# Norm and rotary embedding of q and k joined, with wo and rotary tables loaded per layer and a refitted planner, in a two-layer transformer kernel

## The chip, the cores and the metric

The kernel runs on one core of one Trainium2 chip. The metric is device time in microseconds (us), the median of several executions. The engines of the core are TensorE (matmul; PE in the profile, its weight loads PEld), VectorE (DVE), ScalarE (ACT), GpSimd (POOL) and SyncE (SP), which issues nearly all DMA transfers.

## The reference

The input `x` has 8 sequences of 512 tokens and 256 channels, in float32. Three stages follow one another, each on the layer norm of `x`; the first and the last are the same two-layer network with the same weights:

```python
x = x + 0.5 * ffn(layernorm(x))          # two layers
x = x + global_attention(layernorm(x))   # 16 heads of 16, softmax(y y^T / 4) x, then @ weight
x = x + 0.5 * ffn(layernorm(x))          # the same two layers again

def layer(x):                            # DIM 256, 8 heads of 64, window 128
    h = shift_token(x)                   # second half of the channels from the token before
    q, k, v = split(h @ wqkv)            # 3 x 512
    q = l2norm(q) * q_scale; k = l2norm(k) * k_scale     # per head of 64
    q = q*cos*s + rotate_half(q)*sin*s;  k = k*cos/s + rotate_half(k)*sin/s
    o = local_attention(q, k, v)         # own window and the one before, causal
    x = x + o @ wo
    h = layernorm(shift_token(x)) * g + b
    a, gate = split(h @ w1 + b1)         # 2 x 682
    return x + (a * gelu(gate)) @ w2 + b2
```

## The kernel before, in words

**Streams.** Each of the 8 sequences is a block of 512 tokens, cut into 4 tiles of 128. A block passes twice through the two layers, once before and once after the global attention. Two streams (`k` = 0 and 1) each take 8 such passes in the order of `pairs`, so 16 layers each, 32 in all. A third stream, `global_stream`, does the 16 global heads of each block once its first pass is done. The streams are Python generators that record operations between `yield`s; the first stream starts `LAG` = 6 yields ahead of the second. One layer has 12 yields of attention and 6 of the gated network (`glu`).

**One layer's attention.** `front(t)` makes q, k and v of tile t: three matmuls with `wqkv`, a copy of each from PSUM on ScalarE, and for q and k apart the square (ScalarE), the sum per head and a maximum (VectorE), the power -0.5 (GpSimd, in `rn`), two products with the sine table for the rotated halves (GpSimd, in `t2`), the product with the cosine table, the sum of both, and for k the product with its norm (VectorE). q's norm is applied later, as the scale of the exponential. `scores(t)` multiplies q with the keys of the own and the previous tile, in two groups `g` of 4 heads; VectorE adds the mask and takes the peak, ScalarE takes the exponential and its sum, and the result `pg` is divided by the sum. `values(t)` multiplies it with v, `project(t)` with `wo`. The program order is front(0), then for each t: scores(t), project(t-1), front(t+1), values(t).

**Near and far.** Before the products, q and k and then the probabilities must be transposed. In a stream's first and last pass ("near") TensorE does it, through PSUM. In the six passes between ("far", `FAR and 0 < n < len(blocks) - 1`) VectorE transposes blocks of 32 x 32 and a round trip through DRAM moves the blocks (`turned_far`, `turned_quarters`); there are 24 far layers with 96 tiles and 8 near ones with 32. Scores and values are matmuls of 64 rows that run side by side in the array.

**The order of work.** Nothing is issued as it is recorded. `Plan` records every operation, prices it (`cost`: how long the engine is held, and when the result is there), and `order` writes one list schedule for all engines: of the operations that can start first on an engine, the one of the lowest rank (its place in the recording) goes first, with a bonus of `STICK` ranks for a TensorE operation in the same array mode, and `MODE` ns charged for a change of it. Buffers are rings: a tile takes a slot when its first user is placed, and its slot comes free after its last one, so the planner decides the waits for buffers too. DMAs share one modelled `pipe` of 170 GB/s. The engines then run their own lists in order. As every operation goes through a recorder, nearly all of them have one line (L369) in the profile, and must be told apart by their tiles.

**Buffers and weights.** `wqkv`, `wo` and the rotary tables (times `qk_scales`) of both layers are loaded at the start and stay in SBUF; `w1`, `ends` and `w2` have one buffer and are loaded again for each step by `load_glu`. `qn` (q or k of a tile) has two buffers of 512 numbers per partition and stream; `glu` uses them too.

Of the kernel before, what the change touches and what calls it, by code (L numbers as in the profile page):

```python
# [15 lines left out]
P = 128  # L16
B, N, D = 8, 512, 256
NT = N // P
# [151 lines left out]
def elements(a):  # L170
    n = 1
    for d in a.shape[1:]:
        n *= d
    return n


class Plan:
# [55 lines left out]
    def cost(self, op):  # L233

        if op.engine == "tensor":

            lanes, op.mode = {}, "whole"
            for name, args, kw in op.calls:
                lane, t = 0, 109.0
                if name == "matmul":  # L240
                    a = kw["lhsT"]
                    lane, t = (a.region()[0], args[0].region()[0]), 2 * max(0.842 * elements(kw["rhs"]), 0.852 * a.shape[1])
                    k, m = a.shape
                    op.mode = "fours" if k <= 32 else "quarters" if k <= 64 and m <= 64 else "halves" if k <= 64 else "columns" if m <= 64 else "whole"
                lanes[lane] = lanes.get(lane, 0.0) + t
            busy = max(lanes.values())
            return busy, busy + 170
        name, args, kw = op.calls[0]
        n = max(elements(a) for a in (*args, *kw.values()) if hasattr(a, "shape"))
        if name == "dma_start":  # L250
            return 580.0, 2300.0
        if op.engine == "scalar":
            if name == "activation":
                op.mode = {AF.Exp: "exp", AF.Gelu: "gelu"}.get(args[2])
                busy = 70 + 0.82 * n + (105 if "bias" in kw else 0)
                return (busy + 93, busy + 310) if "accum_out" in kw else (busy, busy + 110)
            return 70 + 0.81 * n, 175 + 0.81 * n
        if op.engine == "vector":
            if name == "tensor_tensor_reduce":
                return 90.0 + n, 250.0 + n  # L260
            if name == "bn_stats":
                return 70.0 + n, 150.0 + n
            return 90 + 1.035 * n, 170 + 1.035 * n
        if name == "memset":
            return 80 + 0.85 * n, 100 + 0.85 * n
        if ALU.pow in args:
            return 350.0 + 157 * n, 400.0 + 157 * n
        return 210 + 1.98 * n, 250 + 1.98 * n

    def order(self):  # L270
# [19 lines left out]
        pipe = 0.0  # L290
# [17 lines left out]
        while len(order) < len(self.ops):  # L308
# [31 lines left out]
            if op.calls[0][0] == "dma_start":  # L340
                a = op.calls[0][2]["out"]
                pipe = max(pipe, op.start + 2000.0) + elements(a) * a.shape[0] * 4 / 170
                op.end = pipe + 300
# [32 lines left out]
def macaron(ctx: ExitStack, tc: tile.TileContext, x, weight, wqkv, wo, w1, w2, b2, vecs, qk_scales, rotary, out):  # L376
# [16 lines left out]
    def load_attention(l):  # L393

        wq = wpool.tile([P, 2, 3 * INNER], F32, tag=f"wqkv{l}", name=f"wqkv{l}")
        for part in range(3):
            cols = slice(part * INNER, (part + 1) * INNER)
            nc.sync.dma_start(out=wq[:, :, cols], in_=wqkv[l, :, cols].rearrange("(k p) f -> p k f", p=P))
        o = wpool.tile([P, NPAIR, D], F32, tag=f"wo{l}", name=f"wo{l}")
        nc.sync.dma_start(out=o, in_=wo[l].rearrange("(k p) f -> p k f", p=P))  # L400
        return wq, o
# [23 lines left out]
    attention_weights = [load_attention(0)]  # L425
    glu_weights = [load_glu(0)]
    attention_weights.append(load_attention(1))
    tabs, vec = [], []
    for l in range(DEPTH):
        tab = const.tile([P, NT, 2, 2, DH], F32, tag=f"tab{l}", name=f"tab{l}")  # L430
        nc.scalar.dma_start(out=tab.rearrange("p t a s d -> p (t a s d)"), in_=rotary)
        sc = zpool.tile([P, 2, 2, DH], F32, tag=f"z{l}", bufs=2, width=N + 1)
        nc.scalar.dma_start(out=sc.rearrange("p a s d -> p (a s d)"), in_=qk_scales[l : l + 1, :].partition_broadcast(P))
        ve = const.tile([P, NVEC], F32, tag=f"vec{l}", name=f"vec{l}")
        nc.scalar.dma_start(out=ve, in_=vecs[l])
        vec.append(ve)
        for t in range(NT):
            nc.gpsimd.tensor_mul(tab[:, t], tab[:, t], sc)
        tabs.append(tab)
# [19 lines left out]
    nhalf = const.tile([P, HEADS], F32, tag="nhalf")  # L459
# [69 lines left out]
    def quarter_buffers():  # L529

        zeros = work.tile([P, 2 * P], F32, tag="t2", bufs=2, width=N)
# [24 lines left out]
    def later(k):  # L556

        if k not in later_of:
            zeros = work.tile([1, P], F32, tag="t2", bufs=2, width=N)
# [6 lines left out]
    def attention(k, y, l, far):  # L566
        wqkv_sb, wo_sb = attention_weights[l]
# [4 lines left out]
        v = {}  # L572
# [3 lines left out]
        def front(t):  # L576
# [4 lines left out]
            tb = tabs[l][:, t]  # L581
            pair = []
            for part in range(3):
# [6 lines left out]
                if part == 2:  # L590
                    vt = work.tile([P, INNER], F32, tag=f"v{k}", bufs=3)
                    nc.scalar.copy(vt, ps)
                    v[t] = vt
                    continue


                qk = work.tile([P, HEADS, 2, half], F32, tag=f"qn{k}", bufs=2)
                flat = qk.rearrange("p h a d -> p (h a d)")
                nc.scalar.copy(flat, ps)
                sq = work.tile([P, HEADS, DH], F32, tag="sq", bufs=1)  # L600
                nc.scalar.activation(sq.rearrange("p h d -> p (h d)"), flat, AF.Square)
# [28 lines left out]
        def scores(t, pair, rn):  # L630
# [21 lines left out]
            for g in range(2):  # L652
# [16 lines left out]
                with plan.together():  # L669
                    for i in range(2):  # L670
                        keys = kT[:, 2 * g + i].rearrange("p j k -> p (j k)")
                        for q, to, ks in sorted(pieces, key=lambda piece: piece[1].start - piece[1].stop):
                            for par in range(2):
# [3 lines left out]
                                )  # L677
                heads = slice(4 * g, 4 * g + 4)
# [53 lines left out]
        def values(t, probs):  # L732
# [25 lines left out]
            if far:  # L758
                for g in range(2):
                    with plan.together():  # L760
                        for i in range(2):
# [3 lines left out]
                            )  # L765
            else:
# [40 lines left out]

    def glu(k, y, step, xb, far):
# [3 lines left out]
        if far:  # L812
            sh = work.tile([P, NT, P], F32, tag=f"qn{k}", bufs=2)
# [40 lines left out]
        for m in range(FULL):  # L854
# [4 lines left out]
            else:  # L859
                u = work.tile([P, N], F32, tag=f"qn{k}", bufs=2)  # L860
# [14 lines left out]
        u = work.tile([P, N], F32, tag=f"qn{k}", bufs=2)  # L875
# [49 lines left out]
    def stream(k, blocks):  # L925

        for n, (b, second) in enumerate(blocks):
# [211 lines left out]
```

## Time and profile before

| | |
|---|---|
| median of 3 runs | 3949.23 us (3947.79 to 3949.27) |
| the profiled execution's own time | 3952.0 us |
| its span, first to last instruction | 3950.1 us |
| mean granted TensorE clock | 0.994 |
| instructions | 72878 |
| DMA | 400.74 MB, mean 101 GB/s |

A page of the profile gives the busy time of each engine and its share of the span, the span in 40 slices, the DMA queues, the chain of waits that ended last, and the groups of instructions. A group names engine, operation, tiles (`out<-in`), shapes and count, then busy time in us and the mean of one in ns, and behind the second bar the idle time before it and what ended it. A table of stretches gives, for each from:to in us, its length, the busy time of the engines with instruction counts, the granted clock and the DMA share. A line of the timeline gives start, duration, engine, tiles, shape and count.

### The profile page before, as it was taken

How to read it: one execution, taken by the hardware profiler on the slowest of the kernel's cores; microseconds unless marked ns; L12 is line 12 of the kernel's file. 1: busy time of each engine (PE TensorE's matmuls, PEld its weight loads, DVE VectorE, ACT ScalarE, POOL GpSimd, SP SyncE). 2: the span in 40 equal slices, each digit the busy share in tenths (PEclk: the TensorE clock that was granted, in tenths of full speed). 3: DMA queues.
4: the chain of work that ended last, by engine and by line, in shares of the span. 5: the costliest groups of instructions: out<-in, count | busy, mean ns of one | idle time of the engine just before them, and what ended most of it. 6: DMA issues, size and time to landing. Idle time of an engine off the chain costs nothing.

```text
span 3950.1 us, 72878 instructions
## 1 busy us (share of the span) xinstructions
PE 3878.5 (98%) x26240; PEld 2659.5 (67%) x26240; DVE 2447.9 (62%) x6888; ACT 1766.9 (45%) x4548; POOL 1233.7 (31%) x1132
## 2 busy tenths in 40 slices
PE   8999999999999999999999999999999999999998
PEld 4566776766767667677676776767767667686665
DVE  7676655667566665674765747657466565535674
ACT  5565534535344353452443534535335353324564
POOL 6242323424133341341422405324133242103240
PEclk9999999999999999999999999999999999999999
DMA  3000543534435344253442534525335244110000
GB/s 116 1 24 27 155 135 104 150 98 140 129 104 153 93 128 143 88 165 92 128 138 94 155 104 130 159 91 156 91 116 157 81 143 134 61 33 9 1 24 11
DMA packets 437644, 400.74 MB, mean 101 GB/s; under 512 B 53954, under 2 KB 379172, under 8 KB 437284
## 3 DMA queue, kind: packets, MB, share of 16 engines
q1 hardware_dynamic: 436420, 394.76, 33.5%
q8 instruction: 208, 3.41, 0.4%
q10 hardware_dynamic: 864, 1.33, 0.1%
q14 instruction: 152, 1.25, 0.1%
HBM read 235.49 MB, written 143.66 MB: 96 GB/s over the span
## 4 chain that ended last, share of the span: by engine, by line
PE 81%; DVE 5%; issue 2%; ACT 2%; POOL 1%; DMA 0%; SPq 0%; DVEq 0%; POOLq 0%; ACTq 0%
PE psum_bank L369 81%; ACT work_p L369 2%; DVE work_p L369 2%; DVE work_qn L369 1%; DVE small_ss L369 1%; POOL small_rn L369 0%; POOL work_t L369 0%; ACT work_both L369 0%; DVE work_xw L369 0%; DVE small_bnst L369 0%; SPq L369 0%; DVE work_both L369 0%; DVE work_o L369 0%; DVE xpool_x L369 0%; POOL small_rstd L369 0%
## 5 line engine op out<-in xcount | busy, mean ns | idle before, releaser
L369 PE MATMUL psum_bank<-work_xw,work_e 128*128 128x256 f32 x4096 | 960.0, 385 | 3.0 <-ACT work_e L369 1.9
L369 PEld LDWEIGHTS psum_bank<-work_xw,work_e 128*128 128x128 f32 x4096 | 765.8, 191 | 199.0 <-issue 47.2
L369 PE MATMUL psum_bank<-wpool_wqkv,zpool_z 128*128 128x512 f32 x1536 | 712.2, 603 | 2.7 <-ACT work_v L369 2.0
L369 ACT ACTIVATE work_p<-work_p,small_nmax,small_rn 128x192 f32<-128x192 f32 (+2 forms) x1024 | 543.7, 533 | 324.2 <-DVE small_nmax L369 213.7
L369 POOL TENSOR_TENSOR work_t<-work_qn,const_tab 128x256 f32<-128x256 f32 x512 | 397.4, 797 | 590.3 <-ACT work_qn L369 503.5
L369 PE MATMUL psum_bank<-zpool_z,wpool_w 128*128 128x512 f32 x1280 | 558.9, 595 | 1.5 <-DVE zpool_z L369 1.5
L369 POOL TENSOR_TENSOR small_rn<-small_ss,const_nhalf 128x8 f32<-128x8 f32 x256 | 484.4, 1893 | 149.8 <-DVE small_ss L369 141.6
L369 POOL TENSOR_TENSOR work_p<-work_p,small_ri 128x768 f32<-128x768 f32 (+1 forms) x192 | 264.4, 1378 | 778.9 <-DVE small_ri L369 371.9
L369 ACT ACTIVATE work_e<-psum_bank 128x512 f32<-128x512 f32 x512 | 298.3, 596 | 420.4 <-PE psum_bank L369 403.9
L369 PE MATMUL psum_bank<-work_wa,work_gz 128*128 128x256 f32 x2048 | 477.6, 381 | 5.9 <-DVE work_gz L369 3.9
L369 PEld LDWEIGHTS psum_bank<-wpool_wqkv,zpool_z 128*128 128x128 f32 x1536 | 284.8, 192 | 288.1 <-issue 266.4
L369 PEld LDWEIGHTS psum_bank<-zpool_z,wpool_w 128*128 128x128 f32 x1280 | 243.5, 191 | 301.8 <-issue 273.7
L369 PEld LDWEIGHTS psum_bank<-work_wa,work_gz 128*128 128x128 f32 x2048 | 385.3, 190 | 78.3 <-issue 14.7
L369 DVE SCALAR_TENSOR_TENSOR xpool_x<-psum_bank,gsmall_rinv,xpool_x 128x256 f32<-128x256 f32 x512 | 242.2, 474 | 283.6 <-PE psum_bank L369 281.2
L369 ACT COPY work_qn<-psum_bank 128x512 f32<-128x512 f32 x256 | 148.4, 582 | 327.1 <-PE psum_bank L369 263.8
L369 DVE SCALAR_TENSOR_TENSOR work_p<-psum_bank,const_vec,work_p 128x512 f32<-128x512 f32 x128 | 95.7, 749 | 278.1 <-PE psum_bank L369 226.9
L369 PE MATMUL psum_bank<-wpool_wo,work_o 128*128 128x256 f32 x1024 | 244.9, 383 | 6.4 <-DVE work_o L369 6.2
L369 PE MATMUL psum_bank<-wpool_w,work_p 128*128 128x256 f32 x1024 | 243.2, 380 | 0.0
L369 DVE COPY work_xw<-psum_bank 128x512 f32<-128x512 f32 x256 | 173.8, 680 | 108.4 <-PE psum_bank L369 107.9
L369 DVE TENSOR_REDUCE small_ss<-work_sq 128x8 f32<-128x512 f32 x256 | 172.2, 673 | 109.0 <-ACT work_sq L369 108.1
L369 PEld LDWEIGHTS psum_bank<-wpool_wo,work_o 128*128 128x128 f32 x1024 | 191.4, 190 | 56.7 <-DVE work_o L369 16.1
L369 ACT ACTIVATE work_p<-psum_bank,const_vec 128x512 f32<-128x512 f32 x128 | 87.9, 687 | 296.6 <-PE psum_bank L369 288.0
(89 smaller groups left out, 4943.3 us busy)
## 6 DMA issues: line engine op xcount, KB each, us to landing
work_p<-dram_quarters SPq DMA_DIRECT2D x576, 128.0 KB
dram_quarters<-work_p SPq DMA_DIRECT2D x288, 192.0 KB
dram_turned<-work_both SPq DMA_DIRECT2D x96, 512.0 KB
work_both<-dram_turned SPq DMA_DIRECT2D x384, 128.0 KB
work_wa<-in_weight_dram SPq DMA_DIRECT2D x128, 256.0 KB
wpool_w<-in_w_dram SPq DMA_DIRECT2D x48, 640.0 KB
work_hT<-work_gz SPq DMA_DIRECT2D x512, 32.0 KB
dram_turned<-work_p SPq DMA_DIRECT2D x48, 256.0 KB
```

The source lines that it names most:

```text
L369: getattr(getattr(nc, op.engine), name)(*map(real, args), **{k: real(a) for k, a in kw.items()})
```

## The change

1. In `front`, q and k go into one tile `qk` of 1024 numbers per partition; the square, sum, maximum, rotated products, power, cosine product and addition are each issued once for both. The last product with the norm stays on k alone. `qn` still has two buffers, each twice as large, `t2` one instead of two; `glu` uses one `qn` buffer for its last two hidden tiles.
2. `wo` and the scaled rotary table have one buffer each. The scaled tables are written to DRAM at the start; when the second stream ends a layer's attention, `load_wo` and `load_tab` for the next layer are recorded.
3. In far layers, the scores of tile t > 0 are recorded as after both groups of the values of tile t-1.
4. `cost` has new constants, distinguishes more forms, and `order` prices DMAs at 330 GB/s and keeps at most 8 of them in flight.

```diff
         name, args, kw = op.calls[0]
         n = max(elements(a) for a in (*args, *kw.values()) if hasattr(a, "shape"))
         if name == "dma_start":
-            return 580.0, 2300.0
+            source = kw["in_"]
+            far = isinstance(source, View) and source.tile.ring.space == DRAM
+            return (560.0 if len(source.shape) > 3 and far else 450.0), 2400.0 if far else 1900.0
         if op.engine == "scalar":
+            base = 60 if args[1].tile.ring.space == PSUM else 100
             if name == "activation":
                 op.mode = {AF.Exp: "exp", AF.Gelu: "gelu"}.get(args[2])
-                busy = 70 + 0.82 * n + (105 if "bias" in kw else 0)
-                return (busy + 93, busy + 310) if "accum_out" in kw else (busy, busy + 110)
-            return 70 + 0.81 * n, 175 + 0.81 * n
+                busy = base + 0.82 * n + (105 if "bias" in kw else 0)
+                return (busy + 92, busy + 280) if "accum_out" in kw else (busy, busy + 105)
+            return base + 0.81 * n, base + 105 + 0.81 * n
         if op.engine == "vector":
             if name == "tensor_tensor_reduce":
-                return 90.0 + n, 250.0 + n
+                return 86.0 + n, 190.0 + n
             if name == "bn_stats":
-                return 70.0 + n, 150.0 + n
-            return 90 + 1.035 * n, 170 + 1.035 * n
+                return 60.0 + n, 145.0 + n
+            pointers = sum(isinstance(u, View) and elements(u) == 1 for u in args[1:])
+            busy = 70 + 1.035 * n + (55 if pointers and name == "scalar_tensor_tensor" else 27 * pointers)
+            return busy, busy + 85
         if name == "memset":
             return 80 + 0.85 * n, 100 + 0.85 * n
         if ALU.pow in args:
-            return 350.0 + 157 * n, 400.0 + 157 * n
-        return 210 + 1.98 * n, 250 + 1.98 * n
+            return 248.0 * n - 10, 248.0 * n + 30
+        busy = 140 + (2.14 if n <= 2 * P else 1.67) * n
+        return busy, busy + 45
 
     def order(self):
 
...
-        pipe = 0.0
+        pipe, flying = 0.0, []
...
             op.end = op.start + op.done
             if op.calls[0][0] == "dma_start":
                 a = op.calls[0][2]["out"]
-                pipe = max(pipe, op.start + 2000.0) + elements(a) * a.shape[0] * 4 / 170
-                op.end = pipe + 300
+                pipe = max(pipe, op.start + op.done - 400) + elements(a) * a.shape[0] * 4 / 330
+                op.end = pipe + 400
+                flying = sorted(flying + [op.end])[-8:]
+                if len(flying) == 8:
+                    free[e] = max(free[e], flying[0])
             for x in op.opens:
                 _, x.slot = x.ring.free.pop(0)
                 x.ring.open(x.stream, x.turn)
...
-        o = wpool.tile([P, NPAIR, D], F32, tag=f"wo{l}", name=f"wo{l}")
+        return wq
+    def load_wo(l):
+        o = wpool.tile([P, NPAIR, D], F32, tag="wo")
-        return wq, o
+        return o
...
+    output_weights = [load_wo(0)]
-    tabs, vec = [], []
+    scaled, vec = [], []
+    tabs = [const.tile([P, NT, 2, 2, DH], F32, tag="tab")]
-        tab = const.tile([P, NT, 2, 2, DH], F32, tag=f"tab{l}", name=f"tab{l}")
-        nc.scalar.dma_start(out=tab.rearrange("p t a s d -> p (t a s d)"), in_=rotary)
+        tab = work.tile([P, NT, 2, 2, DH], F32, tag="p1", bufs=2) if l else tabs[0]
+        flat = tab.rearrange("p t a s d -> p (t a s d)")
+        nc.scalar.dma_start(out=flat, in_=rotary)
...
         vec.append(ve)
         for t in range(NT):
             nc.gpsimd.tensor_mul(tab[:, t], tab[:, t], sc)
-        tabs.append(tab)
+        d = dram.tile([P, NT * 2 * 2 * DH], F32, tag=f"tab{l}")
+        nc.sync.dma_start(out=d, in_=flat)
+        scaled.append(d)
+    def load_tab(l):
+        tab = const.tile([P, NT, 2, 2, DH], F32, tag="tab")
+        nc.sync.dma_start(out=tab.rearrange("p t a s d -> p (t a s d)"), in_=scaled[l])
+        return tab
 
 
 
...
-            zeros = work.tile([1, P], F32, tag="t2", bufs=2, width=N)
+            zeros = work.tile([1, P], F32, tag="t2", bufs=1, width=2 * N)
-    def attention(k, y, l, far):
-        wqkv_sb, wo_sb = attention_weights[l]
+    def attention(k, y, step, far):
+        l = step % DEPTH
+        wqkv_sb, wo_sb = attention_weights[l], output_weights[step]
-        v = {}
+        v, latest = {}, []
...
-            tb = tabs[l][:, t]
-            pair = []
+            tb = tabs[step][:, t]
+            qk = work.tile([P, 2, HEADS, 2, half], F32, tag=f"qn{k}", bufs=2)
...
                             ps, lhsT=z[:, tok], rhs=wqkv_sb[:, c, part * INNER : (part + 1) * INNER], start=(c == 0), stop=(c == 1)
                         )
                 if part == 2:
-                    vt = work.tile([P, INNER], F32, tag=f"v{k}", bufs=3)
-                    nc.scalar.copy(vt, ps)
-                    v[t] = vt
-                    continue
-                qk = work.tile([P, HEADS, 2, half], F32, tag=f"qn{k}", bufs=2)
-                flat = qk.rearrange("p h a d -> p (h a d)")
-                nc.scalar.copy(flat, ps)
-                sq = work.tile([P, HEADS, DH], F32, tag="sq", bufs=1)
-                nc.scalar.activation(sq.rearrange("p h d -> p (h d)"), flat, AF.Square)
-                nc.vector.reduce_sum(ss[:, part], sq, axis=AX.X)
-                nc.vector.tensor_scalar_max(ss[:, part], ss[:, part], 1e-24)
-                t2 = work.tile([P, HEADS, 2, half], F32, tag="t2", bufs=2)
-                for a in range(2):
-                    nc.gpsimd.tensor_mul(
-                        t2[:, :, a, :],
-                        qk[:, :, 1 - a, :],
-                        tb[:, 1, part, a * half : (a + 1) * half].unsqueeze(1).to_broadcast([P, HEADS, half]),
-                    )
-                nc.gpsimd.tensor_tensor(rn[:, part], ss[:, part], nhalf, ALU.pow)
-                qf = qk.rearrange("p h a d -> p h (a d)")
-                nc.vector.tensor_mul(qf, qf, tb[:, 0, part].unsqueeze(1).to_broadcast([P, HEADS, DH]))
-                nc.vector.tensor_add(qk, qk, t2)
-                if part == 1:
-                    nc.vector.tensor_mul(qf, qf, rn[:, 1].unsqueeze(2).to_broadcast([P, HEADS, DH]))
-                pair.append(qk)
+                    v[t] = work.tile([P, INNER], F32, tag=f"v{k}", bufs=3)
+                    nc.scalar.copy(v[t], ps)
+                else:
+                    nc.scalar.copy(qk[:, part].rearrange("p h a d -> p (h a d)"), ps)
+            sq = work.tile([P, 2 * HEADS, DH], F32, tag="sq", bufs=1)
+            nc.scalar.activation(sq.rearrange("p h d -> p (h d)"), qk.rearrange("p s h a d -> p (s h a d)"), AF.Square)
+            flat = ss.rearrange("p s h -> p (s h)")
+            nc.vector.reduce_sum(flat, sq, axis=AX.X)
+            nc.vector.tensor_scalar_max(flat, flat, 1e-24)
+            t2 = work.tile([P, 2, HEADS, 2, half], F32, tag="t2", bufs=1)
+            for a in range(2):
+                nc.gpsimd.tensor_mul(
+                    t2[:, :, :, a, :],
+                    qk[:, :, :, 1 - a, :],
+                    tb[:, 1, :, a * half : (a + 1) * half].unsqueeze(2).to_broadcast([P, 2, HEADS, half]),
+                )
+            nc.gpsimd.tensor_tensor(rn.rearrange("p s h -> p (s h)"), flat, nhalf, ALU.pow)
+            qf = qk.rearrange("p s h a d -> p s h (a d)")
+            nc.vector.tensor_mul(qf, qf, tb[:, 0].unsqueeze(2).to_broadcast([P, 2, HEADS, DH]))
+            nc.vector.tensor_add(qk, qk, t2)
+            nc.vector.tensor_mul(qf[:, 1], qf[:, 1], rn[:, 1].unsqueeze(2).to_broadcast([P, HEADS, DH]))
+            pair = [qk[:, part] for part in range(2)]
             if far:
 
                 both = work.tile([P, 1, 4, 2 * NPAIR, half], F32, tag="both", bufs=2, width=2 * N)
...
                                 nc.tensor.matmul(
                                     sps[par][q, i, to], lhsT=qT[rows, 2 * g + i, q], rhs=keys[rows, ks], start=True, stop=True
                                 )
+                if far and t > 0:
+                    plan.ops[-1].after.update(latest)
                 heads = slice(4 * g, 4 * g + 4)
 
                 if far:
...
                                 2 * g + i,
                                 lambda par, own, rows, q: probs[g][rows, own * (nk - 1), q.start // 32 : q.stop // 32, 2 * i + par, :],
                             )
+                    latest[g:] = [plan.ops[-1]]
             else:
                 turned = []
                 for n in range(NPAIR + 2):
...
             yield
         project(NT - 1, o)
 
+        if k == 1 and step + 1 < DEPTH * len(pairs):
+            output_weights.append(load_wo((step + 1) % DEPTH))
+            tabs.append(load_tab((step + 1) % DEPTH))
     def glu(k, y, step, xb, far):
         l = step % DEPTH
         w1_sb, ends_sb, w2_sb = glu_weights[step]
 
         if far:
-            sh = work.tile([P, NT, P], F32, tag=f"qn{k}", bufs=2)
+            sh = work.tile([P, NT, P], F32, tag=f"qn{k}", bufs=2, width=2 * N)
             tokens = later(k)
             for tiles in (slice(0, NT - 1), slice(NT - 1, NT)):
                 rows = tokens[1 + tiles.start * P : 1 + tiles.stop * P, :]
...
-                u = work.tile([P, N], F32, tag=f"qn{k}", bufs=2)
+                last = work.tile([P, 2, N], F32, tag=f"qn{k}", bufs=2)
+                u = last[:, 0]
...
-                yield from attention(k, y, l, far)
+                yield from attention(k, y, step, far)
```

More of the change, by code (lines that the diff above doesn't have):

```diff
@@ L458, in macaron @@
     make_identity(nc, ident)
-    nhalf = const.tile([P, HEADS], F32, tag="nhalf")
+    nhalf = const.tile([P, 2 * HEADS], F32, tag="nhalf")
     nc.gpsimd.memset(nhalf, -0.5)
@@ L529, in quarter_buffers @@
     def quarter_buffers():
-        zeros = work.tile([P, 2 * P], F32, tag="t2", bufs=2, width=N)
+        zeros = work.tile([P, 2 * P], F32, tag="t2", bufs=1, width=2 * N)
         nc.gpsimd.memset(zeros, 0.0)
@@ L873, in glu @@
                 yield
-        u = work.tile([P, N], F32, tag=f"qn{k}", bufs=2)
+        u = last[:, 1]
         us.append(u)
```

## The prediction

> **What bounds the kernel now.** I read the page first (busy shares, slices, chain of waits), then the span cut into stages, then TensorE's timeline, then the groups of instructions by form.
>
> ```profile
> PE 3878.5 (98%) x26240; PEld 2659.5 (67%) x26240; DVE 2447.9 (62%) x6888; ACT 1766.9 (45%) x4548; POOL 1233.7 (31%) x1132
> ```
>
> TensorE is busy for 3878.5 of 3950.1 us; the chain of waits gives it 81%. The change adds and removes no matmul. Only three things can then move the end: idle time of TensorE (71.6 us), its clock, and what the order of its matmuls costs. The stages (columns: TensorE, weight loads, VectorE, ScalarE, GpSimd, granted clock, DMA share, GB/s):
>
> ```profile
> 25.00:420.00 395.00, 379.02 (x2815) 240.48 (x2817) 278.38 (x797) 236.76 (x544) 142.42 (x134) 0.99 0.11 34
> 420.00:3600.00 3180.00, 3165.21 (x20981) 2207.66 (x20974) 1937.89 (x5431) 1330.09 (x3567) 979.43 (x874) 1.00 0.40 118
> 3600.00:3905.00 305.00, 289.60 (x2315) 186.28 (x2313) 208.49 (x599) 192.03 (x426) 98.25 (x93) 0.98 0.03 10
> ```
>
> In the long middle stage (blocks 1 to 6 of each stream, global heads beside them) TensorE idles 14.8 us in 3180. In the two outer stages (first and last blocks, whose attention is turned on TensorE and has no global heads to fill gaps) it idles 16.0 and 15.4 us. The rest lies before 25 us and after 3905 us. There one gap also shows the clock:
>
> ```profile
> 3865.67 17.43 PE L369 MATMUL psum_bank<-zpool_z,wpool_w 128*128 128x512 f32 x40
> ...
> 3909.08 2.52 PE L369 MATMUL psum_bank<-const_ident,work_p 128*128 128x128 f32 x8 [3.10 <-DVE work_p L369]
> 3912.19 20.35 PE L369 MATMUL psum_bank<-zpool_z,wpool_w 128*128 128x512 f32 x40 [0.58 <-DVE zpool_z L369]
> ```
>
> The same 40 matmuls take 17.43 us, and 20.35 us behind a gap of 3.10 us: the gap costs 2.9 us again. Such dips also stand in the outer stages, where VectorE or ScalarE is full:
>
> ```profile
> 260.00:270.00 10.00, 10.00 (x88) 6.72 (x86) 7.29 (x14) 4.48 (x9) 6.71 (x8) 0.71 0.01 2
> 3810.00:3820.00 10.00, 7.39 (x47) 3.71 (x43) 9.97 (x25) 5.40 (x16) 6.92 (x5) 0.78 0.00 1
> ```
>
> The last cost is the order. Scores and values run as 64-row matmuls, the rest with 128 rows:
>
> ```profile
> 1002.07 0.88 PE L369 MATMUL psum_bank<-work_kT,work_qT 64*64 64x192 f32 x16
> 1002.88 3.70 PE L369 MATMUL psum_bank<-wpool_wqkv,zpool_z 128*128 128x512 f32 x8
> 1006.42 3.62 PE L369 MATMUL psum_bank<-work_xw,work_e 128*128 128x256 f32 x16
> 1009.96 0.90 PE L369 MATMUL psum_bank<-work_p,work_v 64*64 64x128 f32 x32
> ...
> 1013.79 0.90 PE L369 MATMUL psum_bank<-work_p,work_v 64*64 64x128 f32 x32
> 1014.50 1.52 PE L369 MATMUL psum_bank<-work_kT,work_qT 64*64 64x128 f32 x64
> 1015.96 1.98 PE L369 MATMUL psum_bank<-wpool_wqkv,zpool_z 128*128 128x512 f32 x4
> ```
>
> One group of values alone holds TensorE 0.83 us (1009.96 to 1010.79). One such group with two of scores behind it takes 2.17 us (1013.79 to 1015.96), where three alone would take 2.48: each joint saves 0.16 us. Besides, by the starts in the timeline, a 128x256 matmul holds TensorE 216 ns before one of its own kind and 309 ns before a 64-row one: 0.09 us more per visit. I take 0.3 us for a visit saved (a first wide matmul after a visit is often some 0.1 us late as well). I count 469 visits to matmuls of 64 or 16 rows: 140 us in all.
>
> **The change, part by part.** *Fronts joined (128 fronts).* The rows they rest on:
>
> ```profile
> L369 DVE TENSOR_TENSOR work_qn<-work_qn,const_tab 128x512 f32<-128x512 f32 x256 | 183.3, 716 | 17.5 <-POOL work_t L369 17.0
> L369 DVE TENSOR_REDUCE small_ss<-work_sq 128x8 f32<-128x512 f32 x256 | 172.2, 673 | 109.0 <-ACT work_sq L369 108.1
> L369 DVE TENSOR_TENSOR work_p<-work_p,small_ri 128x1024 f32<-128x1024 f32 x48 | 60.5, 1260 | 0.6
> L369 POOL TENSOR_TENSOR small_rn<-small_ss,const_nhalf 128x8 f32<-128x8 f32 x256 | 484.4, 1893 | 149.8 <-DVE small_ss L369 141.6
> L369 POOL TENSOR_TENSOR work_t<-work_qn,const_tab 128x256 f32<-128x256 f32 x512 | 397.4, 797 | 590.3 <-ACT work_qn L369 503.5
> L369 POOL TENSOR_TENSOR work_p<-work_p,small_ri 128x512 f32<-128x512 f32 x48 | 51.6, 1077 | 150.2 <-DVE small_ri L369 135.7 <-DVE small_nmax L369 12.9 <-DVE small_ss L369 1.7
> ```
>
> VectorE per front: two multiplies of 716 ns become one of 1260 (the 128x1024 row), the adds and the sums likewise save some 0.15 each, and one of two 250 ns maxima goes: 0.17 + 0.15 + 0.15 + 0.25 = 0.72 us saved. GpSimd: four of 797 ns become two; the 128x512 row gives 1.08 each, doubling gives 1.59 (no saving); I take 1.08, the nearer form: 3.19 to 2.15. The power goes from two of 1893 (8 columns) to one of 16. The 4-column rows stand at 1009 and 1125, so about 0.22 per column and 3.66 for 16, against 3.79. Square: 2 x 631 to about 1.08, by the slope of the exponentials (128x128 481 ns, 128x256 594). Over 128 fronts that is 92 us of VectorE, 150 us of GpSimd and 23 us of ScalarE. In the middle stage these engines are busy 61, 31 and 42%, TensorE covers them, and I cost it at nothing.
>
> The chain gets longer, though. Before, q's chain starts while k is still on TensorE, and GpSimd's queue sets the pace: 2 x (2 x 0.80 + 1.89) + 0.81 for the last multiply = 7.8 us from q's copy. Now all starts at k's copy, 4 x 0.43 = 1.7 us later: Square 1.08, sum 1.2, max 0.25 (beside 2.15 of GpSimd), power 3.66, multiply 0.81 = 7.0, so 8.7 us: 0.9 us later. What queues behind it: in GpSimd's queue the other stream's products, softmax scaling and rstd powers wait behind one power of 3.66 us where two of 1.89 left a gap; on VectorE the transposes and peaks wait behind one op of 1260. Only the 32 fronts of the outer stages have no cover: bounds +14 us (32 x 0.9 over two streams side by side) and -15 (half of those stages' 31 us idle, since VectorE, which gives 32 x 0.72 = 23 us back, is the engine that ends many of their waits). qn's two buffers now hold whole fronts, so a next front need not wait for the transposes of this one; that speaks for the lower half. I take -4.
>
> A rule speaks against this join. GPSIMD Engine Reference, Key points, of the Trainium skill says that GpSimd shares its SBUF interfaces with VectorE and contends with instructions that read two SBUF inputs. The trace may show it: work_t has median 727, slowest 1717 ns. Were every joined product slowed as that slowest one, GpSimd would save nothing; the sum would change by no more than the bounds above.
>
> *Scores behind both groups of values* (72 far tiles with t > 0). I count 106 visits that hold such scores and 45 that hold scores and values together. One visit per tile, always behind a group of values, would be 72 and 72: (106 - 72) + (72 - 45) = 61 visits fewer. Group 0's scores now wait on TensorE for group 1's values, and the softmax, its DMA round trip and the next values wait behind them; other streams and the global heads cover that. Other work of lower rank may still come between, so I take half: 30 x 0.3 = -9 us; bounds -18 (all 61) and +6 (20 visits more, where streams now join by chance).
>
> *wo and tables per layer.* 29 loads more of 512 KB (14 of wo, 15 of tables). On SP each is one issue of 0.37 us, 11 us in all, in a queue that holds 2.6 thousand issues of 0.2 to 0.6 us; 15.2 MB is 3.8% of 400.74 MB. Two writes of 512 KB at the start are off the path. The wait: the table's single buffer comes free when the second stream's last front has read it, and the first stream's next attention must wait for the reload. In the trace at least 45 us lie between (3675 to 3720); for wo at least 58 (3723 to 3781). The first x, 512 KB among other loads, took under 8.8 us. So nothing; without that cover 15 x 8.5 = 128 us.
>
> DMA: Bandwidth & Descriptors, Anatomy of one DMA, of the Trainium skill gives 2.0 us plus bytes over 436 GB/s: an estimate of 3.2 us a load. By it too the load is hidden.
>
> *Planner's model.* Its prices move towards the rows (128x768 scaling 1771 to 1467, row 1478; 8-column power 1656 to 2014, row 1893), by 0.4 us at most and on engines with slack. A DMA lands 0.3 to 1.9 us sooner in it. This redraws the order everywhere; the gain is bounded by the middle's 14.8 us, the loss by the rival below. I take -4, from -15 to +30.
>
> Sum: -4 - 9 - 4 = -17 us: 3952.0 to 3935.0 for a profiled execution. That one lies 2.8 above the median of 3949.2, so I say 3932.
>
> **The rivals.** *A larger gain*: all 61 visits and half the outer idle: -18 - 15 - 10 = -43 us, 3906. For it: the loss of visits is real. Against: the middle is full. *Nothing*: new joints are lost elsewhere, the outer stages stay bound by VectorE: 3949, within 8 us. A measurement of this kernel can tell about 0.2%, 8 us, from no change. *Slower*: the new model prices SP's transfers at 330 GB/s instead of 170 and their landing at 1.9 us for writes. TensorE takes its queue in order; today no wait of TensorE is ended by a DMA, since the old price left slack. With it gone, values stand in the queue before their rows have landed, and all behind them waits. There are 192 far groups: 0.2 us late on average gives +38, less the 17, 3949 + 21 = 3970. It decides from 0.09 us per group (17/192). Against: a visit has other streams' work ahead of it.
>
> **How the numbers follow.** Forecast 0.42, larger gain 0.13, nothing 0.18, slower 0.27; so faster 0.55, same 0.18, slower 0.27. The range runs from a bit past the larger gain (3896) into the slower case (3972).
>
> **What would show it.** Right: TensorE's busy time down by 5 to 15 us with the same matmul count, visits near 440, outer stages' idle under 31 us, the joined GpSimd product near 1.08 us and power near 3.7 us. Wrong: waits of TensorE on a DMA or on work_p in the middle, more dips of the clock, visits at 470 or more, or the first stream's fronts waiting on the table's load.

## Result and the profile after

The changed kernel takes 4077.45 us (median of 4 runs, 4068.07 to 4083.88), against 3949.25 for the kernel before in the same comparison: a ratio of 1.0326, 95% interval 1.0305 to 1.0346, 128 us slower. 3932 was forecast, with a range up to 3972. The mechanism of the rival called *slower* is what happened, at three to six times the price put on it. In an experiment below, changing one number of the planner takes the whole loss back (0.15% faster than the kernel before, 95% interval 0.03 to 0.26%).

The first lines of the page after, and its engine shares in the chain of waits:

```profile
span 4082.1 us, 71586 instructions
PE 3929.9 (96%) x26240; PEld 2699.2 (66%) x26240; DVE 2371.9 (58%) x6376; ACT 1814.0 (44%) x4472; POOL 1162.4 (28%) x748
...
PE 58%; DMA 8%; DVE 8%; ACT 5%; SPq 5%; issue 3%; POOL 1%; DVEq 0%; POOLq 0%; ACTq 0%
```

There are as many matmuls as before, and VectorE and GpSimd do less (76 and 71 us). But TensorE has idled 4082.1 - 3929.9 = 152.2 us, against 71.6: 80.6 of the 132 us between the two spans. The chain of waits, 81% TensorE before, is now 58%, with DMA and SyncE's queue at 8 and 5% where both were near 0. The rest of the 132 us, 51.4, is TensorE busy for longer. Most of that is the clock: the mean granted clock fell from 0.994 to 0.984, and 0.016 x 4082 less 0.006 x 3950 is 42 us. Nine us are left, and 71 visits fewer to narrow matmuls (398 for 469) should, at the prediction's 0.3 us each, have given 21 back. (A visit is an unbroken run of narrow matmuls; the 398 are 272 of 64 or 43 rows and 126 of 16 rows.) Of these 30 us, 17 lie in the values of the far layers, `psum_bank<-work_p,work_v`: counted from one matmul's start to the next, without idle time and at full clock, they hold TensorE for 154.2 us, for 136.8 before. The other 13 I cannot assign to a line.

The table of stretches of the same kernel (TensorE, weight loads, VectorE, ScalarE, GpSimd, granted clock, DMA share, GB/s):

```profile
25.00:420.00 395.00, 380.20 (x2807) 241.49 (x2806) 272.15 (x723) 235.88 (x527) 130.08 (x78) 0.99 0.13 41
420.00:3600.00 3180.00, 3084.81 (x20352) 2142.40 (x20351) 1828.45 (x4960) 1347.93 (x3427) 924.61 (x583) 0.98 0.42 121
```

The first outer stage is as it was (14.8 us idle for 16.0). The middle stage, full before (14.8 us idle), now has 95 us idle in the same 3180 us, at a clock of 0.98. What TensorE waits for, in total us, times, and the longest:

```profile
PE psum_bank L381 <- DMA work_p<-dram_quarters: 56.6, 63, 3.5
PE psum_bank L381 <- DVE ypool_y L381: 17.1, 8, 13.5
PE psum_bank L381 <- DVE work_p L381: 11.5, 16, 3.3
```

The largest waits before, of which none was for a DMA:

```profile
PE psum_bank L369 <- DVE ypool_y L369: 15.9, 4, 12.3
PE psum_bank L369 <- ACT work_both L369: 9.3, 16, 1.4
```

`work_p<-dram_quarters` is the last hop of the probabilities' round trip, in front of the values. One such place in TensorE's timeline, SyncE's timeline at that time, and the same ten us as a stretch:

```profile
1292.11 1.16 PE L381 MATMUL psum_bank<-work_hT 16*128 16x512 f32 x8
1296.72 0.69 PE L381 MATMUL psum_bank<-work_p,work_v 64*64 64x128 f32 x4 [3.45 <-DMA work_p<-dram_quarters]
1298.00 2.06 PE L381 MATMUL psum_bank<-work_p,work_v 64*64 64x128 f32 x32 [0.59 <-DMA work_p<-dram_quarters]
```
```profile
1290.50 0.46 SPq L381 DMA_DIRECT2D const_tab<-dram_tab  x1
1291.05 5.20 SPq L381 DMA_DIRECT2D work_p<-dram_quarters  x8
```
```profile
1290.00:1300.00 10.00, 5.96 (x56) 3.78 (x52) 2.74 (x7) 5.53 (x21) 1.47 (x1) 0.77 1.02 250
```

The 8 reads issue from 1291.05 to 1296.25, behind a reload of the table. The values stand at the head of TensorE's queue from 1293.27, stop it for 3.45 us and again for 0.59, and the matmuls behind them stand too. In these ten us VectorE and GpSimd are busy for 2.74 and 1.47 us, the DMA engines are full (1.02) at 250 GB/s, and the clock granted falls to 0.77.

The clock's records show 9 stretches at half clock before (47.8 us) and 28 after (136.5 us), of 3.4 us or a multiple. TensorE was busy for 40.4 us of the first and 124.4 us of the second, which costs half of that: 20 and 62 us, again 42 more. In 19 of the 28 a wait of TensorE for a DMA lies in the 8 us before the stretch; before, in none of the 9. TensorE: Matmul & The Clock Gate (What's actually happening) of the Trainium skill has a window of about 3.4 us by which the clock is halved; the lengths agree. By that page the half clock comes after at least one whole idle window; here only one of the 28 has a single idle gap that long in the 8 us before it, so shorter gaps were enough. What exactly fills or empties such a window, no run here shows.

### The profile page after: what moved, and what is told of

It reads as the page before. It is cut to its first block, busy times and chain, and to the rows that moved or that the text cites. A ratio compares the mean times of both kernels' runs of the same rounds, so it can differ in the third digit from the quotient of the medians.

```text
span 4082.1 us, 71586 instructions
## 1 busy us (share of the span) xinstructions
PE 3929.9 (96%) x26240; PEld 2699.2 (66%) x26240; DVE 2371.9 (58%) x6376; ACT 1814.0 (44%) x4472; POOL 1162.4 (28%) x748
## 4 chain that ended last, share of the span: by engine, by line
PE 58%; DMA 8%; DVE 8%; ACT 5%; SPq 5%; issue 3%; POOL 1%; DVEq 0%; POOLq 0%; ACTq 0%
PE psum_bank L381 58%; SPq L381 5%; ACT work_p L381 3%; DMA work_p<-dram_quarters 3%; DVE work_p L381 3%; DMA dram_quarters<-work_p 2%; DVE work_qn L381 1%; ACT L381 1%; DMA work_p<-dram_turned 1%; DMA dram_turned<-work_both 1%; DMA work_both<-dram_turned 1%; DVE ypool_y L381 0%; DMA dram_turned<-work_p 0%; DVE xpool_x L381 0%; POOL work_t L381 0%
## 5 line engine op out<-in xcount | busy, mean ns | idle before, releaser
L381 POOL TENSOR_TENSOR small_rn<-small_ss,const_nhalf 128x16 f32<-128x16 f32 x128 | 467.5, 3653 | 230.6 <-DVE small_ss L381 228.1
L381 POOL TENSOR_TENSOR work_p<-work_p,small_ri 128x768 f32<-128x768 f32 (+1 forms) x192 | 275.5, 1438 | 867.2 <-DVE small_ri L381 480.1
L381 POOL TENSOR_TENSOR work_t<-work_qn,const_tab 128x512 f32<-128x512 f32 x256 | 329.3, 1305 | 661.2 <-ACT work_qn L381 548.6
L381 PE MATMUL psum_bank<-work_p,work_v 64*64 64x64 f32 (+1 forms) x5376 | 186.2, 259 | 66.5 <-DMA work_p<-dram_quarters 56.6
L381 PEld LDWEIGHTS psum_bank<-work_p,work_v 64*64 64x64 f32 x5376 | 151.9, 139 | 142.7 <-issue 102.5
L381 DVE STREAM_TRANSPOSE work_p<-work_p 128x768 f32<-128x768 f32 (+2 forms) x216 | 202.2, 937 | 73.4 <-POOL work_p L381 72.9
L381 DVE TENSOR_REDUCE small_ss<-work_sq 128x16 f32<-128x1024 f32 x128 | 155.1, 1212 | 154.3 <-ACT work_sq L381 154.1
```

Source lines behind the costliest of these rows:

```text
L381: getattr(getattr(nc, op.engine), name)(*map(real, args), **{k: real(a) for k, a in kw.items()})
```

## Experiments

Three theories were put up. **M**: the planner's new prices leave no slack, so values stand in TensorE's queue before they have landed. **L**: scores behind both groups of values lengthen each tile's chain. **J**: the joined fronts or the reloads cost. All ratios are to the kernel before, run beside each.

### First: which part (r1 to r4)

r1: the changed kernel with every price of before, that is `cost()` of before, 170 GB/s and no limit of 8.

> The changed kernel with all the planner's prices of before (joined fronts, loads per layer and scores behind both values stay). Theory M (the new prices leave no slack, so TensorE stands at values whose DMA has not landed): back to 3930 to 3970 us, TensorE's waits on DMA work_p<-dram_quarters under 10 us. Theory L (scores behind both groups of values lengthen each tile's chain): stays at 4040 to 4080. Theory J (joined fronts or reloads): stays at 4040 to 4080 too.

r2: the kernel before with only the new prices, that is the new `cost()`, 330 GB/s and the limit of 8.

> The kernel before with only the planner's new prices and its limit of 8 DMAs. Theory M: slower, 4030 to 4080 us, with waits of TensorE on DMA. Theories L and J: 3930 to 3960, since none of their parts is in it.

r3: the changed kernel with the old prices of DMAs alone.

```diff
-            return (560.0 if ... else 450.0), 2400.0 if far else 1900.0
+            return 580.0, 2300.0
...
-                pipe = max(pipe, op.start + op.done - 400) + elements(a) * a.shape[0] * 4 / 330
-                op.end = pipe + 400
-                flying = sorted(flying + [op.end])[-8:]
-                if len(flying) == 8:
-                    free[e] = max(free[e], flying[0])
+                pipe = max(pipe, op.start + 2000.0) + elements(a) * a.shape[0] * 4 / 170
+                op.end = pipe + 300
```


> The changed kernel with the old prices of DMAs alone (580 and 2300 ns, 170 GB/s, no limit of 8); the new prices of the engines stay. Theory M, if it is the DMA's price: 3940 to 3990 us. If it is the engines' prices: 4050 to 4080. Theories L and J: 4040 to 4080.

r4: the changed kernel without the order of scores.

```diff
-                if far and t > 0:
-                    plan.ops[-1].after.update(latest)
```


> The changed kernel without the edit that puts far scores behind both groups of values. Theory L: back to 3930 to 3980 us. Theories M and J: 4060 to 4100, and visits to 64-row matmuls rise again from 272.

| run | us | ratio (95%) | TensorE's wait on `work_p<-dram_quarters`, us | visits |
|---|---|---|---|---|
| r1 | 4020.40 | 1.0185 (1.0156 to 1.0215) | 0.4 | 403 |
| r2 | 4042.66 | 1.0242 (1.0212 to 1.0271) | 36.3 | 371 |
| r3 | 4006.91 | 1.0151 (1.0122 to 1.0181) | none | 390 |
| r4 | 4081.27 | 1.0339 (1.0309 to 1.0369) | 61.6 | 393 |

In r2 the largest wait of TensorE is the one of the changed kernel:

```profile
PE psum_bank L381 <- DMA work_p<-dram_quarters: 36.3, 48, 2.5
```

L falls: without its edit the time stays, and so do the visits. M is supported by r2: prices alone, with the same operations in another order, cost 94 us. From r2 to r4 the joined fronts and the reloads come in, and 39 us more; from r4 to the changed kernel the order of scores, and 4 us less, which two runs of 4079 and 4084 us do not tell from nothing. So under these prices J is not nothing. And r1 and r3 missed: the old prices take the DMA waits away and leave 59 to 72 us, so something else in the changed program does not suit the old prices.

### Second: reloads, joined fronts, and slack by itself (r5 to r8)

r5: the kernel before with only `wo` and the tables loaded per layer (part 2 of the change), with the old prices.

> The kernel before with only the loads per layer (wo and the tables in one buffer each); fronts apart, old prices, old order of scores. If the reloads are hidden, as predicted: 3940 to 3960 us. If they cost what the old prices with joined fronts cost (r1): 4005 to 4030.

r6: r1 without the order of scores; against r5 it has the joined fronts, with their buffers, and nothing else.

> Joined fronts and loads per layer with the old prices and without the scores-behind-values edit. Against r5 it differs by the joined fronts alone. Theory J (the joined fronts cost): 4005 to 4035, as r1. If the reloads or the order of scores were the cost in r1: under 3985.

r7: the changed kernel, with one number changed.

```diff
-                op.end = pipe + 400
+                op.end = pipe + 1900
```


> The changed kernel, only that the planner takes every DMA to land 1.5 us later (400 to 1900 ns after its bytes); nothing on the chip changes but the order. Theory M: 3990 to 4030 us, TensorE's waits on DMA work_p<-dram_quarters from 57 us to under 10. If slack is not the cause: 4060 to 4100.

r8: the kernel before with the new prices of DMAs only.

```diff
-            return 580.0, 2300.0
+            return (560.0 if ... else 450.0), 2400.0 if far else 1900.0
...
-                pipe = max(pipe, op.start + 2000.0) + elements(a) * a.shape[0] * 4 / 170
-                op.end = pipe + 300
+                pipe = max(pipe, op.start + op.done - 400) + elements(a) * a.shape[0] * 4 / 330
+                op.end = pipe + 400
```


> The kernel before with only the new prices of DMAs (no limit of 8, old prices of the engines). Theory M by the DMA's price: 4010 to 4050 us, close to r2's 4043. If the engines' new prices made r2 slow: 3940 to 3970.

r5 takes 3953.28 us (1.0021, 1.0009 to 1.0032): under the old prices the reloads cost 7 us, not nothing, and not the loss. r6 takes 4014.93 (1.0174, 1.0144 to 1.0203): under the old prices the joined fronts cost 62 us. r8 takes 3997.10 (1.0129, 1.0085 to 1.0172), a little under the range that M gave, 28.5 us of it standing at `work_p<-dram_quarters`: the DMA's prices without the limit of 8 make half of r2's loss. The rest came with the engines' new prices and the limit, which no run separates here.

r7 takes 3941.10 us (0.9985, 0.9974 to 0.9997). The same program as the changed kernel, ordered as if each DMA landed 1.5 us later, is 136 us faster than it and a little faster than the kernel before. That was more than theory M expected. Its page and its waits:

```profile
PE 3860.0 (98%) x26240; PEld 2656.1 (67%) x26240; DVE 2375.0 (60%) x6376; ACT 1764.4 (45%) x4434; POOL 1160.9 (29%) x748
```
```profile
PE psum_bank L381 <- DVE work_p L381: 11.4, 16, 3.3
...
PE psum_bank L381 <- DMA work_p<-dram_quarters: 7.1, 10, 1.6
```
```profile
420.00:3600.00 3180.00, 3156.58 (x21078) 2211.89 (x21071) 1883.37 (x5059) 1329.80 (x3486) 928.47 (x587) 1.00 0.43 122
```

The DMA waits are down from 56.6 to 7.1 us, the middle stage idles 23 us, and the clock is 1.00 there (0.997 over the span). GpSimd's and VectorE's work is that of the changed kernel. So the joined fronts do not make a slow kernel by themselves: the 39 us that they and the reloads cost from r2 to r4 are gone with the prices that leave slack. ScalarE's `ACT_TABLE_LOAD`s, 1.28 us each, rose with the change from 100 to 152. They do not decide the time either: r2 has 100 of them in 4043 us, r5 has 138 in 3953.

### Third: the dose (r9, r10, r15, r16)

The same line with other numbers, for r9, r10, r15 and r16 in this order.

```diff
-                op.end = pipe + 400
+                op.end = pipe + 1100   # then 3400, 1500, 2300
```

> As r7 with 0.7 us instead of 1.5 us more until a DMA lands in the planner (400 to 1100 ns). Slack theory: between the changed kernel and r7, 3960 to 4010 us, waits of TensorE on DMA work_p<-dram_quarters between 7 and 57 us. If r7 was a lucky order: anything, without regard to the slack.

> As r7 with 3.0 us instead of 1.5 us more (400 to 3400 ns). Slack theory: no waits on DMA are left, 3920 to 3950 us. If too much caution also costs, as with the old prices in r3: 3960 to 4010.

> As r7 with 1.1 us instead of 1.5 us more until a DMA lands. Slack theory: between r9 (0.7 us, 3989) and r7 (1.5 us, 3941): 3945 to 3980 us.

> As r7 with 1.9 us instead of 1.5 us more until a DMA lands. Slack theory: near the optimum, 3925 to 3950 us; the waits of TensorE on DMA under r7's 7 us.

| more until a DMA lands | us | ratio (95%) | wait on `work_p<-dram_quarters`, us | visits |
|---|---|---|---|---|
| 0 (the change) | 4077.45 | 1.0326 (1.0305 to 1.0346) | 56.6 | 398 |
| 0.7 us (r9) | 3989.09 | 1.0109 (1.0080 to 1.0139) | 29.7 | 404 |
| 1.1 us (r15) | 3969.25 | 1.0054 (1.0038 to 1.0070) | 16.9 | 410 |
| 1.5 us (r7) | 3941.10 | 0.9985 (0.9974 to 0.9997) | 7.1 | 406 |
| 1.9 us (r16) | 3943.27 | 0.9990 (0.9980 to 1.0000) | 4.4 | 409 |
| 3.0 us (r10) | 3956.54 | 1.0022 (1.0010 to 1.0033) | none | 407 |

The time falls step by step to a flat bottom near 1.5 to 1.9 us, which lucky orders would hardly do. Past it, the waits on DMA are gone and caution costs 15 us; r10 lies between the two ranges that were given for it.

From 0 to 1.5 us these waits fall by 49.5 us and the time by 136. The two profiled executions, 144.7 us apart, show where the rest is. TensorE's waits on all DMAs fall by 54.9 us and its other idle time by 19.9; its busy time at half clock fell from 124.4 to 17.0 us, worth 53.7; and the far values hold it for 136.8 us again instead of 154.2, worth 17.4. These add up to 145.9, one more than the difference.

One thing stays open. The later landing also makes the planner's limit of 8 hold SyncE back sooner, and no run has the slack without the limit. So how much is due to values that are placed later, and how much to DMAs that are issued in another order, is not shown.

### Fourth: the parts under good prices (r11, r12)

r11 is r2 with r7's line: fronts apart, nothing reloaded. r12 is r7 without the order of scores. The first edit is in both, the second in r12 alone.

```diff
-                op.end = pipe + 400
+                op.end = pipe + 1900
...
-                if far and t > 0:
-                    plan.ops[-1].after.update(latest)
```

> The kernel before with the planner's new prices and 1.5 us more until a DMA lands; fronts apart, no reloads, old order of scores. Slack theory: r2's 4043 falls to 3930 to 3960 us. Against r7 (3941) it shows what the joined fronts are worth under good prices: 0 to 15 us if they are worth what was forecast.

> As r7 without the edit that puts far scores behind both groups of values. If the edit is worth its visits: 3945 to 3955 us and 430 or more visits against r7's 406. If the planner joins them anyway: within 5 us of r7.

r11: 3952.69 us (1.0016, 1.0004 to 1.0027). r12: 3948.10 (1.0003, 0.9991 to 1.0014), with 417 visits for r7's 406, where 430 or more were expected. With slack in the prices, joined fronts and reloads together show 5 us (r11 to r12) and the order of scores 7 (r12 to r7). The intervals of neighbours overlap, so neither step is shown by itself; those of the two ends, r11 and r7, do not overlap, so the 12 us of all three together are.

### Fifth: which old price held the slack (r13, r14, r17, r18)

r13 is the changed kernel with the first edit alone, r14 is r3 with its reverse, r17 is r13 with the second edit, and r18 is r3 with the second edit's reverse.

```diff
-  ... + elements(a) * a.shape[0] * 4 / 330
+  ... + elements(a) * a.shape[0] * 4 / 170
...
-                flying = sorted(flying + [op.end])[-8:]
-                if len(flying) == 8:
-                    free[e] = max(free[e], flying[0])
```

> The changed kernel with the old rate of 170 GB/s alone; all other new prices stay. If the old rate was the slack: 3950 to 4010 us, waits of TensorE on DMA work_p<-dram_quarters under 15 us. If the fixed time was the slack: 4040 to 4080.

> r3 (old fixed times of DMAs, no limit of 8) with the new rate of 330 GB/s alone. If the old rate was the slack: 4040 to 4090 us and waits on DMA as in the changed kernel. If the fixed time was the slack, and the rate only made r3's plan slow: 3940 to 3980.

> r13 (old rate of 170 GB/s, the rest new) without the planner's limit of 8 DMAs in flight. If the missing limit is what made r3 slow (the modelled queue grows without bound and the order waits for it): 3995 to 4025 us. If the old fixed times did: 3955 to 3975.

> r3 (old DMA prices in the changed kernel) with the limit of 8 DMAs in flight kept. If the missing limit made r3 slow: 3955 to 3980 us. If the old fixed times did: 3995 to 4020.

r13: 3965.47 us (1.0047, 1.0031 to 1.0063), 0.5 us of waits on those DMAs. r14: 4012.94 (1.0169, 1.0148 to 1.0189), 32.6 us of them. With the limit of 8 kept, the old rate alone takes 112 of the 128 us back. But r14 lies between the two ranges given for it, neither as slow as without slack nor as fast as with it, so the old fixed times had some slack too. r17: 4017.59 (1.0179, 1.0144 to 1.0214). r18: 3994.68 (1.0121, 1.0091 to 1.0150), between the two ranges given for it. Without the limit the old rate takes back only 60 us (r17), though the waits on those DMAs are as small there (0.5 us). The limit of 8 is worth 52 us beside the old rate (r13 against r17), and only 12 beside all old DMA prices (r3 against r18), where 29 us stay over r13. So r3's loss is partly the missing limit and partly the fixed times. Why those suit the joined fronts so badly, while the kernel before lived well with both, stays open. The waits of r3 name no single place:

```profile
PE psum_bank L376 <- DVE xpool_x L376: 10.8, 7, 5.2
PE psum_bank L376 <- ACT work_both L376: 10.6, 15, 3.2
PE psum_bank L376 <- DVE work_e L376: 10.4, 3, 9.9
PE psum_bank L376 <- DVE work_gz L376: 10.4, 6, 4.4
```

## Why the prediction was wrong, point by point

**The planner's model: the step that failed.** It was put at -4 us, from -15 to +30; by itself it is +94 (r2). (Joined fronts and reloads, taken at -4 and nothing, add 39 from r2 to r4, and the order of scores takes 4 off: 129 in all, for 128 measured.) The argument was that its prices move towards the rows, by 0.4 us at most on engines with slack, and the gain is bounded. But for DMAs nothing in the shown rows said what a price should be, and "0.3 to 1.9 us sooner" compares the two prices of one DMA alone, without others beside it. The time from a DMA's issue to the end of the wait for it, in the changed kernel's trace: for the 192 KB write to `dram_quarters` 2.9 us (median of 61 waits of SyncE; 90th percentile 4.2), where the new price gives 2.5, and for the 128 KB read back 3.2 us (63 waits of TensorE; 90th percentile 4.6), where it gives 2.8. Somebody stood waiting for these, so they are the late ones; but all 124 took longer than the new price, while the old one, 3.5 us for a write and 3.1 for a read alone, lay above 45 of the 61 writes and 8 of the 63 reads, and its 170 GB/s adds more time for every DMA in front. The late ones stood in a crowd: from 1 us before to 2.5 us after their issue the DMA engines were 85% busy for the slowest third of the reads (4.3 us on average) and 59% for the quickest third (3.1 us).

Between 420 and 3600 us the kernel moves at most 269 GB/s in a ten-us stretch with the DMA engines 80% busy or more. The new rate of 330 is passed only at the start, where loads of up to 640 KB come in (369 GB/s from 10 to 20 us). So the new price was too low for a DMA in a crowd, and the old one, with its lower rate, covered part of that. DMA: Bandwidth & Descriptors (Anatomy of one DMA) of the Trainium skill gives 2.0 us and bytes over 436 GB/s for a DMA that GpSimd issues, by which 128 KB would take an estimated 2.3 us; SyncE issues those here, and the measured 3.2 decides.

**The rival "slower".** Right in mechanism and sign of evidence (no wait on a DMA before, one in front of the values after), with a chance of 0.27. Its price failed: 0.2 us late per far group, +38, less 17. The waits alone are 56.6 + 5.4 us, the latter on `work_p<-dram_turned`, so 0.3 us per far group. The clock adds 42 and the broken-up values 17, and the delay spreads: TensorE's other idle time grew by 18.5. The prediction's own first lines had shown a gap of 3.10 us costing 2.9 us more by the clock, and the rival's price left that factor out.

**Joined fronts.** The durations hold. The rows after (VectorE, ScalarE, GpSimd):

```profile
L381 DVE TENSOR_TENSOR work_qn<-work_qn,const_tab 128x1024 f32<-128x1024 f32 x128 | 157.0, 1226 | 19.6 <-POOL work_t L381 19.2 <-DMA wpool_wqkv<-in_wqkv_dram 0.3
L381 DVE TENSOR_REDUCE small_ss<-work_sq 128x16 f32<-128x1024 f32 x128 | 155.1, 1212 | 154.3 <-ACT work_sq L381 154.1
L381 ACT ACTIVATE work_sq<-work_qn 128x1024 f32<-128x1024 f32 x128 | 135.5, 1059 | 8.1 <-DVE small_ss L381 4.8
L381 POOL TENSOR_TENSOR work_t<-work_qn,const_tab 128x512 f32<-128x512 f32 x256 | 329.3, 1305 | 661.2 <-ACT work_qn L381 548.6 <-issue 89.2 <-DMA dram_quarters<-work_t 17.8
L381 POOL TENSOR_TENSOR small_rn<-small_ss,const_nhalf 128x16 f32<-128x16 f32 x128 | 467.5, 3653 | 230.6 <-DVE small_ss L381 228.1
```

1226 for 1260, 1212 for 1200, 1059 for 1080, and 3653 for 3660 ns. Only the joined product was off: 1305 ns, where I took 1080 of the ends 1080 and 1590, and GpSimd saved 71 us instead of 150. That they cost or gain little at the end holds under prices with slack (r11 to r12). What was not foreseen is that the same fronts cost 62 us under the old prices (r5 to r6), and 39 us with the reloads under the new ones (r2 to r4). Their length is nearly the same in all kernels that have them (r1, r6 and r7: 1208 to 1213 ns for the sums, 3.5 to 3.7 us for the power), so the order that they bring about must decide; which place in it costs the time is not shown.

**Scores behind both groups.** Taken at -9 us for 30 visits. Visits fell by 71, but not by this edit: r4 has 393 without it, and r2, the kernel before with new prices, 371. The attribution failed. Under prices with slack the edit gives 11 visits and perhaps 7 us (r12 to r7).

**Loads per layer.** Taken at nothing; r5 says 7 us. No instruction waits for the table's load in the changed kernel's trace, and the first use of a reloaded table comes 60 us or more after the issue of its load: the cover held. In the stretch above, though, a reload stands straight in front of the values' reads. The cover was reckoned for who reads the table, not for who shares the queue; what that sharing costs, no run shows.

**The outer stages** were taken at -4: the first has 14.8 us idle for 16.0, the last (3732 to 4037 us, as long as the one before) 17.5 for 15.4. Together they gained nothing.

## What to carry to other kernels

A list schedule worked out ahead for engines that run in order needs prices with margin on whatever others can delay, and the margin can sit where nobody calls it one: a rate of 170 GB/s that looked plainly wrong was, together with the limit of 8, enough to take 112 of 128 us back. When such a model is fitted to a trace, fit shared resources to their late cases and engines to their medians, and try the margin as a dose. Price a wait in TensorE's queue with what it does to the clock and to everything queued behind it; here 50 us of waits went together with 136 us.

## What the runs showed of the hardware

The 192 KB write landed within 2.7 us in the quickest tenth of the cases where SyncE waited for it and after 4.2 us or more in the slowest, in one kernel. Full DMA engines moved 250 GB/s in a stretch of the middle and 369 GB/s in one at the start. Half-clock stretches came 28 times in a kernel whose TensorE was busy 96% of the time, and all but one without a single idle gap of 3.4 us in the 8 us before: short gaps in a dense stream are enough.
